# PSUM tiles of one bank for the weighted sums and the final apply, and a re-dealt tail, in a fused attention-convolution and whitening kernel

## The chip, the cores and the metric

The kernel runs on one core of one Trainium2 chip. The core has five engines with a queue of instructions each, which run side by side and wait for each other by semaphores: PE (TensorE, matrix multiplications and transposes), DVE (VectorE), ACT (ScalarE), POOL (GpSimd) and SP (SyncE, used here to issue transfers). PE writes its results to PSUM, which DVE and ACT read; a PSUM bank holds 512 float32 values on each of the 128 partitions. Transfers between the chip's memory (DRAM) and the on-chip SBUF run on 16 DMA engines.

The metric is the time of one execution on the device in microseconds (us). Everything is computed in float32.

## The reference

```python
def _L0_conv_ref(x, w1, b1, w2, b2):          # x: 4 x 256 x 64 x 64
    k = conv(x, w1, padding=6, rhs_dilation=2) + b1      # 7x7 taps, 256 -> 128 channels
    k = conv(k, w2) + b2                                 # 1x1, 128 -> 49
    attn = softmax(k, axis=1)                            # 49 weights for each pixel
    xp = pad(x, 6)
    shifts = stack([xp[:, :, 2*u:2*u+64, 2*v:2*v+64] for u in range(7) for v in range(7)], axis=1)
    return einsum('bkchw,bkhw->bchw', shifts, attn)      # y: 4 x 256 x 64 x 64

def _L1_conv_ref(X, weight, bias):            # 4 groups of 64 channels
    x = X.transpose(1, 0, 2, 3).reshape(4, 64, -1)       # m = 4*64*64 pixels
    xc = x - x.mean(-1, keepdims=True)
    Sigma = 1e-5 * I + einsum('gdm,gem->gde', xc, xc) / m
    rTr = 1.0 / trace(Sigma);  Sigma_N = Sigma * rTr;  P = I
    for _ in range(5):
        P = 1.5 * P - 0.5 * (P @ P @ P) @ Sigma_N
    return (P * sqrt(rTr)) @ xc * weight + bias          # back in NCHW order
```

The first layer computes 49 weights for every pixel and takes the weighted sum of the 49 neighbours. The second needs the mean and covariance of the whole first layer's result before it can write a single output value.

## The kernel before, in words

**Sub-images.** With a dilation of 2, pixels of even and odd rows and columns don't meet. The kernel splits the four images by row parity and column parity into 16 sub-images `n` (0 to 15; `LAST` is 15) of 32 x 32 pixels and 256 channels. The channels are held as two halves `cc` of 128.

**The long first part (to about 310 us and beyond).** The 7x7 convolution is done by a fast transform: DVE forms transformed inputs (`xh`, with the pivot update `ct<-rb`), PE multiplies them (`cv<-xh,wr`, L603, the largest group of the profile; direct rows at L770), DVE and ACT collect (`pv`, `zz`). Softmax follows on ACT and DVE. ACT copies the weights into `zt` (L1126), POOL's queue stores them to DRAM as `sd` (L1145), and SP's queue loads them back as banded matrices `band` and `bandz`, so that a weighted sum becomes a matrix multiplication.

**One sub-image.** `make_blocks` transposes x on PE (L1251) and copies the blocks to SBUF (`xb`, L1282, with edges `xbz`, L1273). `weighted_sum` multiplies blocks by bands into `y` in PSUM (L1320), in two halves of 16 rows, each in five pieces for each `cc`. `store_y` adds a shift and stores y into the place of x (`slot`; ACT at L1342, DVE at L1338). `turn_y` transposes the stored y back (PE, L1399) and copies it to `yt` (ACT, L1409). `moment` multiplies `yt` by itself into the sums `sig` (PE, L1418), from which the covariances come. The methods `first_half` and `second_half` interleave these steps for two neighbouring sub-images, and a plan interleaves them with the convolution of later images.

**The last sub-image** goes in parts, so that channel half 0 is whole early: `store_part` (ACT L1360, DVE L1356), `turn_part` (PE L1368, copies L1377) and `moments_part`. What remains of channel half 1 lies in a list, `units`, of small pieces of PE work.

**Whitening.** `whiten(cc)` is a generator of some eleven steps: trace and mean, then four iterations (the first of the five is in closed form), each of them a multiplication (L1708 through `parts_mm`), a copy `sq` out of PSUM (`evict`), a second multiplication, and DVE's update of `Pm`. The chain for `cc` 0 calls `fill()` between its steps; each call pops a unit onto PE. The chain for `cc` 1 runs later, one step for each tile of the apply loop from tile 4 on (`LEAD`).

**Apply.** 33 output tiles (31 of 512 KB, two half ones at the start): for each, PE multiplies y by the whitening matrix into two PSUM tiles (`parts_mm`, L1708), ACT (L1837) and DVE (L1843) evict one each with scale and shift into `out` (six buffers), and SP issues the transfer (L1849). `bank_pairs` deals the PSUM tiles in turn from three places: pool `ps_y` (one tile of two banks, `apply`), `cv_buf` (two tiles of one bank) and pool `ps_tp` (two of three tiles of one bank).

**Order.** PE's order is the order of the program. On the other engines a scheduler places instructions by priority and by when their inputs come; `high_priority` moves one forward and `issue_after` ties it behind another. Dependences are kept tile by tile. Thus `ps_y`, one buffer of two banks, held both channel halves (or, in `LAST`, both row halves) of y at once.

Of the kernel before, what the change touches and what calls it, by code (L numbers as in the profile page):

```python
# [9 lines left out]
F32 = mybir.dt.float32  # L10
AF = mybir.ActivationFunctionType
# [12 lines left out]
INF = 6  # L24
# [8 lines left out]
def kernel(  # L33
# [71 lines left out]
    ps_tp = ctx.enter_context(tc.tile_pool(name="ps_tp", bufs=3, space=bass.MemoryType.PSUM))  # L105
    ps_y = ctx.enter_context(tc.tile_pool(name="ps_y", bufs=1, space=bass.MemoryType.PSUM))
    ps_sg = ctx.enter_context(tc.tile_pool(name="ps_sg", bufs=1, space=bass.MemoryType.PSUM))
# [702 lines left out]

    acc = ps_y.tile([P, 2, Q8, W], F32, tag="y", name="acc")
    nc.vector.memset(acc, 0.0)
    rows = [(0, br) for br in (1, 2, 3)]
# [40 lines left out]
    def direct0(br, sr):  # L854
        if br in xrs:
            gb = gb5 if br == 5 else gbr
            direct(
                0, br, sr, conv_psum() if br == 5 else acc[:, sr],
                [gb[:, v, :, sr] for v in range(KS)], xrs[br],
            )  # L860
        else:
            u = KS - 1 - 4 * sr - (3 if br == INF else 0)
            w = [tap[:, UPOS[u], v] for v in range(KS)]
            direct(0, br, sr, conv_psum() if br == INF else acc[:, sr], w)

# [96 lines left out]

    direct(1, INF, 0, acc[:, 0], [tap[:, UPOS[3], v] for v in range(KS)])
    prepare(NR0, 1)
# [332 lines left out]
    def weighted_sum(n, half, k, ccs=range(NCC)):  # L1297

        m = PIECES[half][k]
        if n < LAST:  # L1300
            if k == 0:
                y = ps_y.tile([P, NCC, HALF, SW], F32, tag="y", name=f"y_{n}_{half}")
                for cc in ccs:
                    y_ps[n, half, cc] = y[:, cc]
        elif (half, k) == (0, 0):
            y = ps_y.tile([P, 2, HALF, SW], F32, tag="y", name=f"y_{n}_{ccs[0]}")
            for o in range(2):
                y_ps[n, o, ccs[0]] = y[:, o]
        xb = blocks[n, m]
# [34 lines left out]

    y_dve, y_act = {}, {}

    def store_part(half, cc, both=True):

        yt, pc = where(LAST)
        shift = pivots[place(LAST)[1]][:, cc : cc + 1]  # L1350
        ps = y_ps.pop((LAST, half, cc)).rearrange("p r (h c) -> p h r c", h=2)
        for h in range(2):
            o = halves(yt)[:, cc, h, half * HALF : (half + 1) * HALF, bass.ds(pc, TC, 2)]
            with tc.high_priority():
                if h and both:
                    y_dve[LAST, half] = nc.vector.tensor_scalar(  # L1356
                        o, ps[:, h], shift, None, ALU.add
                    )
                else:
                    y_act[0] = nc.scalar.activation(o, ps[:, h], AF.Identity, bias=shift)  # L1360

    def turn_part(half, cc, to=None, on=(nc.scalar.copy, nc.vector.tensor_copy)):

        yt, pc = where(LAST)
        t = tp()
        for k in range(4):
            pe(
                nc.tensor.transpose(  # L1368
                    t[:, k * P : (k + 1) * P],
                    tile_of(yt, cc, 2 * half + k // 2, k % 2, pc),  # L1370
                    turned_by(LAST),
                )
            )
        to = cc if to is None else to
        for k in range(2):
            with tc.high_priority():
                on[k](  # L1377
                    yt_buf[k][:, :, to, :, :GW],
                    t[:, k * C : (k + 1) * C].rearrange("p (h g c) -> p h g c", h=2, c=GW),
                )  # L1380
        turned_part[half, cc] = [yt_buf[k][:, h, to] for k in range(2) for h in range(2)]

    turned_part = {}

    def moments_part(half, cc, pieces=range(4), end=False):

        for k in pieces:
            moment(turned_part[half, cc][k], cc, end and k == 3)

# [270 lines left out]
    sums(0, 0, 3, 4)  # L1660
    store_part(0, 0)
    make_blocks(LAST, 3, y_dve[LAST, 0])
    moments(prev, 1)
    root = work.tile([P, 1], F32, tag="root", name="root")
    with tc.issue_after(y_act[0].ins):
        nc.scalar.activation(root, cmask[:, :1], AF.Sqrt)
    turn_part(0, 0)
    sums(1, 0, 0, 1, 2, 3, 4)
    store_part(1, 0)
    moments_part(0, 0)  # L1670
    turn_part(1, 0)
    sums(0, 1, 0, 1)
# [3 lines left out]
        lambda: sums(0, 1, 2, 3),  # L1676
        lambda: (sums(0, 1, 4), store_part(0, 1, False)),
        lambda: sums(1, 1, 0, 1, 2),
        lambda: sums(1, 1, 3),
        lambda: (sums(1, 1, 4), store_part(1, 1)),  # L1680
        lambda: turn_part(0, 1),
        lambda: turn_part(1, 1, 0, [nc.vector.tensor_copy] * 2),
        lambda: moments_part(0, 1, (0, 1)),
# [29 lines left out]
    def whiten(cc):  # L1713
# [4 lines left out]

        def evict(o, i):
            (nc.vector.tensor_copy if cc else nc.scalar.copy)(o, i)  # L1720

        G = sig[:, cc]
# [10 lines left out]
        nc.vector.tensor_scalar(dg, dg, 1.0 / NPIX, EPS, ALU.mult, ALU.add)  # L1733
        nc.vector.scalar_tensor_tensor(dg, mu, nmu, dg, ALU.mult, ALU.add)
        fill()
# [7 lines left out]
        S = PS[:, 1]  # L1743
        nc.vector.scalar_tensor_tensor(S, G[:, :GW], 1.0 / NPIX, eps, ALU.mult, ALU.add)
        nc.vector.scalar_tensor_tensor(S, t[:, :GW], mu, S, ALU.mult, ALU.add)
# [5 lines left out]
        Pm = PS[:, 0]  # L1751
        nc.vector.scalar_tensor_tensor(Pm, S, -0.5, i15, ALU.mult, ALU.add)
        fill()
        yield

        for it in range(1, T_ITERS):
            t = tp()
            parts_mm(t[:, : 2 * GW], Pm, PS.rearrange("p a c -> p (a c)"))
            sq = rpool.tile([P, 2, GW], F32, tag="sq", name=f"sq{cc}_{it}", bufs=2)
            evict(sq.rearrange("p a c -> p (a c)"), t[:, : 2 * GW])  # L1760
            fill()
            yield
            t = tp()
            parts_mm(t[:, :GW], sq[:, 0], sq[:, 1])
            nc.vector.tensor_scalar(Pm, Pm, 1.5, None, ALU.mult)
            nc.vector.scalar_tensor_tensor(Pm, t[:, :GW], -0.5, Pm, ALU.mult, ALU.add)
            fill()
            yield
# [8 lines left out]
        qi = work.tile([P, 1], F32, tag="qi", name=f"qi{cc}")  # L1777
        nc.vector.reciprocal(qi, q)
        nc.vector.scalar_tensor_tensor(q, qi, rtr, q, ALU.mult, ALU.add)
# [24 lines left out]
    def bank_pairs():  # L1804
        while True:
            t = ps_y.tile([P, 2, NT], F32, tag="y", name="apply")
            yield [t[:, k] for k in range(2)]
            yield cv_buf
            yield [tp(), tp()]
# [3 lines left out]
    for cc in range(NCC):  # L1813
        for b in (3, 2, 1, 0):
# [3 lines left out]
            for k, (r0, nr) in enumerate(rows):  # L1818
# [4 lines left out]
                for pr in range(2):  # L1823
# [5 lines left out]
                        crossed=pr == 1,  # L1829
                    )  # L1830
                if idx > LEAD + 1:
                    next(chains[1], None)
# [51 lines left out]
```

## Time and profile before

| what | value |
|---|---|
| time, median of 3 runs | 682.76 us (682.63, 682.76, 684.98) |
| profiled execution, its own time | 683.23 us |
| its span (first to last instruction) | 681.3 us |
| mean PE clock granted | 0.996 |
| PE busy | 648.7 us, 95% of the span |
| DVE, ACT, POOL busy | 568.4 (83%), 330.4 (48%), 117.2 us (17%) |
| DMA moved | 126.09 MB, mean 185 GB/s |
| output transfers, 512 KB each | 31, 5.0 us from issue to landing in the median |
| first output transfer issued | 635.87 us |

The page's times are microseconds from the start of the span. A line of a timeline reads: start, duration, engine, source line, operation, output<-input, partitions x elements and type, count, and in brackets how long the engine sat idle before it and what ended that. A line of the waits reads: the waiting group <- what it waited for: total, times, longest. The profiled execution is one of its own, and its time lies 0.47 us above the median of the three runs.

### The profile page before, as it was taken

The numbers are of one execution on the slowest core, as the hardware profiler recorded it, in microseconds if no ns is written. First come the engines' busy times: TensorE is split into PE (matmuls) and PEld (weight loads), VectorE is DVE, ScalarE is ACT, GpSimd is POOL, SyncE is SP. The second block draws the span as 40 slices with busy tenths as digits, with TensorE's granted clock in tenths as the row PEclk, the third lists the DMA queues.
The fourth block names the chain that finished last, engine by engine and source line by source line (L and its number), as shares of the span: only waits on it lengthen the run. The fifth ranks groups of instructions, "written<-read, shape, count | busy, mean of one in ns | idle before, by whom it ended". The sixth has DMA issues, their size and how long they took to land.

```text
span 681.3 us, 19062 instructions
## 1 busy us (share of the span) xinstructions
PE 648.7 (95%) x7800; PEld 527.3 (77%) x7800; DVE 568.4 (83%) x1248; ACT 330.4 (48%) x857; POOL 117.2 (17%) x177
## 2 busy tenths in 40 slices
PE   6999999999999999999899999999999999999993
PEld 1439573357899998889899998999899989997421
DVE  2699999899489889999999589989998987634773
ACT  1424340023565565566755555373854656534563
POOL 0000551652213020001022020002220203400000
PEclk9999999999999999999999999999999999999998
DMA  8961999992599979322587484026373325648698
GB/s 318 245 162 67 141 280 349 226 182 33 132 198 222 226 156 361 126 69 74 166 270 250 134 297 166 2 67 190 104 190 109 70 63 138 169 101 362 241 391 357
DMA packets 110607, 126.09 MB, mean 185 GB/s; under 512 B 69255, under 2 KB 91896, under 8 KB 109368
## 3 DMA queue, kind: packets, MB, share of 16 engines
q1 hardware_dynamic: 93528, 69.03, 35.2%
q0 software_dynamic: 10944, 37.57, 21.9%
q10 hardware_dynamic: 6048, 18.27, 8.5%
q8 instruction: 61, 1.00, 0.6%
q14 instruction: 26, 0.21, 0.1%
HBM read 78.78 MB, written 52.36 MB: 192 GB/s over the span
## 4 chain that ended last, share of the span: by engine, by line
PE 66%; DVE 20%; ACT 6%; DMA 4%; issue 2%; POOL 0%; ACTq 0%; SPq 0%; DVEq 0%; POOLq 0%
PE cv L603 22%; PE y L1320 11%; PE cv L770 8%; PE acc L770 8%; PE sig L1418 4%; PE tp L1399 3%; PE tp L1251 3%; DVE pv L352 2%; DVE zz L352 2%; PE cv L251 2%; DVE xh L352 2%; DMA out_dram<-out 2%; DVE ct L352 2%; DVE zz L348 1%; ACT d L1048 1%
## 5 line engine op out<-in xcount | busy, mean ns | idle before, releaser
L603 PE MATMUL cv<-xh,wr 128*49 128x128 f32 x4160 | 232.5, 273 | 0.3 <-ACT pv L614 0.2
L603 PEld LDWEIGHTS cv<-xh,wr 128*49 128x49 f32 x4160 | 226.1, 124 | 3.4 <-issue 1.0
L1145 POOL DMA_DIRECT2D sd<-zt x124 | 65.2, 533 | 334.2 <-ACT zt L1126 268.9
L1320 PE MATMUL y<-band,xb 128*128 128x209 f32 x448 | 94.0, 342 | 5.0 <-ACT xb L1282 2.7
L1320 PEld LDWEIGHTS y<-band,xb 128*128 128x128 f32 x448 | 75.7, 190 | 6.5 <-ACT xb L1282 3.3
L614 ACT COPY pv<-cv 113x486 f32<-113x486 f32 (+2 forms) x60 | 26.0, 433 | 86.4 <-PE cv L603 82.2
L352 DVE SCALAR_TENSOR_TENSOR pv<-pv 113x162 f32<-113x162 f32 x176 | 53.4, 325 | 2.1 <-ACT pv L614 1.3
L1126 ACT COPY zt<-d 32x112 f32<-32x112 f32 (+2 forms) x132 | 38.6, 292 | 15.5 <-DVE d L996 9.9
L1409 ACT COPY yt<-tp 128x512 f32<-128x512 f32 x60 | 35.0, 593 | 19.4 <-PE tp L1399 19.0
L1399 PE MATMUL tp<-ident,slot 128*128 128x128 f32 x240 | 41.5, 296 | 1.2 <-ACT slot L1342 1.2
L1048 ACT ACTIVATE d<-tp,mx 128x49 f32<-128x49 f32 x96 | 27.5, 323 | 28.3 <-DVE mx L1045 28.3
L1251 PE MATMUL tp<-ident,slot 128*128 128x128 f32 x256 | 40.5, 282 | 0.0
L1399 PEld LDWEIGHTS tp<-ident,slot 128*128 128x128 f32 x240 | 34.9, 205 | 6.3 <-issue 3.7
L1418 PE MATMUL sig<-yt 128*64 128x65 f32 x1024 | 38.1, 225 | 1.5 <-ACT yt L1409 1.5
L1251 PEld LDWEIGHTS tp<-ident,slot 128*128 128x128 f32 x256 | 38.2, 204 | 0.2 <-issue 0.2
L1418 PEld LDWEIGHTS sig<-yt 128*64 128x64 f32 x1024 | 33.0, 137 | 6.5 <-ACT yt L1409 2.2
L352 DVE SCALAR_TENSOR_TENSOR xh<-ct 128x512 f32<-128x512 f32 x40 | 26.7, 696 | 10.0 <-PE cv L603 9.8
L1282 ACT COPY xb<-tp 128x512 f32<-128x512 f32 x52 | 30.7, 589 | 8.8 <-PE tp L1251 5.6
L770 PE MATMUL acc<-slot,tap 128*49 128x256 f32 (+7 forms) x224 | 34.7, 468 | 0.0
L770 PEld LDWEIGHTS acc<-slot,tap 128*49 128x49 f32 x224 | 16.1, 123 | 17.9 <-issue 15.5
L147 POOL DMA_DIRECT2D slot<-in_x_dram x12 | 20.4, 1699 | 54.6 <-DVE xh L352 38.2
L348 DVE TENSOR_TENSOR pv<-pv 113x162 f32<-113x162 f32 (+1 forms) x77 | 27.7, 369 | 0.3
(259 smaller groups left out, 1144.4 us busy)
## 6 DMA issues: line engine op xcount, KB each, us to landing
out_dram<-out SPq DMA_DIRECT2D x31, 512.0 KB, 5.0
band<-sd SPq DMA_DIRECT2D x64, 242.0 KB, 3.5
sd<-zt POOLq DMA_DIRECT2D x124, 77.0 KB, 3.1
wr<-gd ACTq DMA_DIRECT2D x14, 588.0 KB, 5.2
wr<-gd ACTq DMA_DIRECT2D x14, 490.0 KB, 4.8
slot<-in_x_dram POOLq DMA_DIRECT2D x12, 512.0 KB, 10.4
ahead<-in_x_dram POOLq DMA_DIRECT2D x12, 512.0 KB, 7.7
spill<-slot POOLq DMA_DIRECT2D x3, 2048.0 KB, 10.7
```

Of the source, the lines that this page charges most:

```text
L348: return in_turn(TT(o, a, b, ALU.subtract))
L352: return in_turn(STT(o, a, f, b, ALU.mult, ALU.add))
L603: nc.tensor.matmul(o, wv[:, sc, sr, cc], xv[bc][:, h * NCC + cc], start=(j == 0), stop=(j == len(terms) - 1), skip_group_check=True,)
L770: nc.tensor.matmul(ps[h * HB : h * HB + KT, :, o0:o1], w[v][:, cc], rhs, start=(j == 0 and k == 0), stop=(j == len(order) - 1), skip_group ...
L1048: nc.scalar.activation(d[:, h, i], t[:, i % NI, h, :KT], AF.Exp, bias=mx[:, i, h : h + 1], accum_out=s[:, h, i : i + 1],)
L1126: ins = nc.scalar.copy(o, i)
L1145: dma = queue.dma_start(bass.AP(tensor=D.tensor, offset=D.offset + h * HS + g * RS, ap=[[LS, TC], [CR * RS, NCH], [1, KS * WS]],), zt[p0 : ...
L1251: nc.tensor.transpose(t[:, h * C + cc * P : h * C + (cc + 1) * P], tile_of(xt, cc, t8, h, pc), turned_by(n),)
L1320: nc.tensor.matmul(y_ps[n, half, cc][:, q0 : q0 + nq, c0:c1], xb[:, cc * P : (cc + 1) * P], rhs, start=(k == 0), stop=(k == len(PIECES[hal ...
L1399: nc.tensor.transpose(t[:, h * C + cc * P : h * C + (cc + 1) * P], tile_of(yt, cc, t8, h, pc), turned_by(n),)
L1409: return nc.scalar.copy(yb.rearrange("p h a g c -> p (h a g) c")[:, :, :GW], t[:, : 2 * C].rearrange("p (e c) -> p e c", c=GW),)
L1418: nc.tensor.matmul(sig[g * GW : (g + 1) * GW, cc], yb[:, g, :GW], yb[:, g], start=(count[0] == 0), stop=end, skip_group_check=True,)
```

## The change

It does five things.

1. `ps_y` has two buffers of one bank instead of one of two. Each y (row half, channel half) and each apply tile of that pool is a tile of its own; so are the two accumulators `acc` of the direct rows.
2. In the last sub-image each bank's y is stored by one engine in one instruction: ACT, and DVE for (1,1). Before, ACT took one half of the columns and DVE the other.
3. A turned block is two transposes in a tile of its own with one copy, not four transposes and two copies by two engines. Each `turn_part` has two parts k; the second is copied by DVE in channel half 0, and all four of channel half 1 by ACT.
4. `units` therefore has 13 entries instead of 11. The chain of `cc` 0 pops the first eleven; the last two, the moments of (1,1), are popped behind the apply tiles 1 and 2.
5. In the whitening chains three small DVE instructions are tied to an order (`traced`, `first`), and the `sq` copies of `cc` 1 go from DVE to ACT.

```diff
-    ps_y = ctx.enter_context(tc.tile_pool(name="ps_y", bufs=1, space=bass.MemoryType.PSUM))
+    ps_y = ctx.enter_context(tc.tile_pool(name="ps_y", bufs=2, space=bass.MemoryType.PSUM))
...
-    acc = ps_y.tile([P, 2, Q8, W], F32, tag="y", name="acc")
-    nc.vector.memset(acc, 0.0)
+    acc = [ps_y.tile([P, Q8, W], F32, tag="y", name=f"acc{sr}") for sr in range(2)]
+    for a in acc:
+        nc.vector.memset(a, 0.0)
...
     def weighted_sum(n, half, k, ccs=range(NCC)):
-        if n < LAST:
-            if k == 0:
-                y = ps_y.tile([P, NCC, HALF, SW], F32, tag="y", name=f"y_{n}_{half}")
-                for cc in ccs:
-                    y_ps[n, half, cc] = y[:, cc]
-        elif (half, k) == (0, 0):
-            y = ps_y.tile([P, 2, HALF, SW], F32, tag="y", name=f"y_{n}_{ccs[0]}")
-            for o in range(2):
-                y_ps[n, o, ccs[0]] = y[:, o]
+        for cc in ccs if k == 0 else ():
+            y_ps[n, half, cc] = ps_y.tile(
+                [P, HALF, SW], F32, tag="y", name=f"y_{n}_{half}_{cc}"
+            )
...
-    def store_part(half, cc, both=True):
+    def store_part(half, cc, on_dve=False):
...
-        ps = y_ps.pop((LAST, half, cc)).rearrange("p r (h c) -> p h r c", h=2)
-        for h in range(2):
-            o = halves(yt)[:, cc, h, half * HALF : (half + 1) * HALF, bass.ds(pc, TC, 2)]
-            with tc.high_priority():
-                if h and both:
-                    y_dve[LAST, half] = nc.vector.tensor_scalar(
-                        o, ps[:, h], shift, None, ALU.add
-                    )
-                else:
-                    y_act[0] = nc.scalar.activation(o, ps[:, h], AF.Identity, bias=shift)
+        i = y_ps.pop((LAST, half, cc)).rearrange("p r (h c) -> p h r c", h=2)
+        o = halves(yt)[:, cc, :, half * HALF : (half + 1) * HALF, bass.ds(pc, TC, 2)]
+        with tc.high_priority():
+            if on_dve:
+                return nc.vector.tensor_scalar(o, i, shift, None, ALU.add)
+            return nc.scalar.activation(o, i, AF.Identity, bias=shift)
 
-    def turn_part(half, cc, to=None, on=(nc.scalar.copy, nc.vector.tensor_copy)):
+    def turn_part(half, cc, k, to=None, on=nc.scalar.copy):
...
         t = tp()
-        for k in range(4):
+        for h in range(2):
             pe(
                 nc.tensor.transpose(
...
-        for k in range(2):
-            with tc.high_priority():
-                on[k](
-                    yt_buf[k][:, :, to, :, :GW],
-                    t[:, k * C : (k + 1) * C].rearrange("p (h g c) -> p h g c", h=2, c=GW),
-                )
+        yb = yt_buf[k][:, :, cc if to is None else to]
+        with tc.high_priority():
+            on(yb[:, :, :, :GW], t[:, :C].rearrange("p (h g c) -> p h g c", h=2, c=GW))
...
-    store_part(0, 0)
-    make_blocks(LAST, 3, y_dve[LAST, 0])
+    stored = store_part(0, 0)
+    make_blocks(LAST, 3)
...
-    turn_part(0, 0)
+    turn_part(0, 0, 0)
+    turn_part(0, 0, 1, on=nc.vector.tensor_copy)
...
-    turn_part(1, 0)
+    turn_part(1, 0, 0)
+    turn_part(1, 0, 1, on=nc.vector.tensor_copy)
...
     units = [
         lambda: sums(0, 1, 2, 3),
-        lambda: (sums(0, 1, 4), store_part(0, 1, False)),
+        lambda: (sums(0, 1, 4), store_part(0, 1)),
         lambda: sums(1, 1, 0, 1, 2),
         lambda: sums(1, 1, 3),
-        lambda: (sums(1, 1, 4), store_part(1, 1)),
-        lambda: turn_part(0, 1),
-        lambda: turn_part(1, 1, 0, [nc.vector.tensor_copy] * 2),
+        lambda: (sums(1, 1, 4), store_part(1, 1, True)),
+        lambda: turn_part(0, 1, 0),
+        lambda: turn_part(0, 1, 1),
+        lambda: turn_part(1, 1, 0, 0),
+        lambda: turn_part(1, 1, 1, 0),
         lambda: moments_part(0, 1, (0, 1)),
         lambda: moments_part(0, 1, (2, 3)),
         lambda: moments_part(1, 1, (0, 1)),
...
-        def evict(o, i):
-            (nc.vector.tensor_copy if cc else nc.scalar.copy)(o, i)
...
-        nc.vector.scalar_tensor_tensor(dg, mu, nmu, dg, ALU.mult, ALU.add)
+        traced = nc.vector.scalar_tensor_tensor(dg, mu, nmu, dg, ALU.mult, ALU.add)
...
-        nc.vector.scalar_tensor_tensor(S, G[:, :GW], 1.0 / NPIX, eps, ALU.mult, ALU.add)
+        with tc.issue_after(traced.ins):
+            nc.vector.scalar_tensor_tensor(S, G[:, :GW], 1.0 / NPIX, eps, ALU.mult, ALU.add)
...
-        nc.vector.scalar_tensor_tensor(Pm, S, -0.5, i15, ALU.mult, ALU.add)
+        first = nc.vector.scalar_tensor_tensor(Pm, S, -0.5, i15, ALU.mult, ALU.add)
...
-            evict(sq.rearrange("p a c -> p (a c)"), t[:, : 2 * GW])
+            nc.scalar.copy(sq.rearrange("p a c -> p (a c)"), t[:, : 2 * GW])
...
-        nc.vector.reciprocal(qi, q)
+        with tc.issue_after(first.ins):
+            nc.vector.reciprocal(qi, q)
...
     def bank_pairs():
         while True:
-            t = ps_y.tile([P, 2, NT], F32, tag="y", name="apply")
-            yield [t[:, k] for k in range(2)]
+            yield [ps_y.tile([P, NT], F32, tag="y", name="apply") for _ in range(2)]
...
+                if idx in (1, 2):
+                    units.pop(0)()
                 if idx > LEAD + 1:
                     next(chains[1], None)
```

## The prediction

> **What bounds the kernel now.** I read the page's totals and slices first, then its chain that ended last, then the waits of PE and the timeline over the last 65 us, where the change does its work, and the windows by stage.
>
> ```profile
> span 681.3 us, 19062 instructions
> ...
> PE   6999999999999999999899999999999999999993
> ...
> DMA  8961999992599979322587484026373325648698
> ...
> PE 66%; DVE 20%; ACT 6%; DMA 4%; issue 2%; POOL 0%; ACTq 0%; SPq 0%; DVEq 0%; POOLq 0%
> ...
> PE y L1320 <- ACT slot L1360: 0.7, 1, 0.7
> ```
>
> PE is at 9 tenths nearly everywhere and its waits are small (the one shown is 0.7 of 681). Only the last slices change the limit: PE falls to 3 and DMA rises to 8. Around 625 to 650 two limits must be kept apart, PE's and the queues'.
>
> ```profile
> 625.88 0.46 PE L1320 MATMUL y<-bandz,xbz 128*128 128x96 f32 x2 [0.67 <-ACT slot L1360]
> ...
> 627.01 0.44 PE L1708 MATMUL tp<-PS 64*64 64x128 f32 x4
> ...
> 628.74 0.44 PE L1708 MATMUL tp<-PS 64*64 64x128 f32 x4
> ...
> 630.72 0.43 PE L1708 MATMUL tp<-PS 64*64 64x128 f32 x4
> ...
> 632.24 0.44 PE L1708 MATMUL tp<-PS 64*64 64x128 f32 x4
> ...
> 633.89 0.41 PE L1708 MATMUL apply<-slot,PS 64*64 64x256 f32 x2
> ...
> 634.70 0.56 ACT L1837 ACTIVATE out<-apply,ab 128x256 f32<-128x256 f32 x1 [0.73 <-PE apply L1708]
> ...
> 635.30 0.54 DVE L1843 TENSOR_SCALAR out<-apply,ab 128x256 f32<-128x256 f32 x1 [0.81 <-ACT out L1837]
> ...
> 635.87 39.74 SPq L1849 DMA_DIRECT2D out_dram<-out  x33
> ```
>
> The last sums on PE, the four whitening iterations of the first channel half (starts 627.01, 628.74, 630.72, 632.24), the first apply tile at 633.89, its two evictions one after the other, and the first output transfer at 635.87. From there:
>
> ```profile
> 630.00:634.70 4.70, 4.62 (x75) 3.54 (x75) 2.63 (x11) 1.04 (x4) 0.00 (x0) 1.00 0.02 3
> ...
> 637.00:639.00 2.00, 1.97 (x20) 0.51 (x16) 1.64 (x3) 1.09 (x2) 0.00 (x0) 1.00 1.04 400
> ...
> 641.00:643.00 2.00, 1.05 (x13) 0.20 (x11) 1.93 (x7) 1.09 (x2) 0.00 (x0) 1.00 1.02 408
> 643.00:645.00 2.00, 2.00 (x24) 0.67 (x20) 1.54 (x5) 1.22 (x3) 0.00 (x0) 1.00 0.95 369
> ...
> 647.00:649.00 2.00, 1.77 (x20) 0.41 (x13) 1.98 (x6) 1.45 (x2) 0.00 (x0) 1.00 0.78 307
> ```
>
> (Columns: stretch, length, busy PE, PEld, DVE, ACT, POOL, then PE clock, DMA share, GB/s.) The output is 16.78 MB; at 408 GB/s a 512 KB tile takes 1.28 us. The queues are idle until 635.87 and then full to the end except where share is under 1: about 0.4 us in 647–649 and about 0.9 in the rest of 637–649, 1.3 in all. So the end is set by the first transfer's start, plus 41 us of data, plus 1.3 us of hunger. A later eviction that is only faster brings nothing.
>
> **The change part by part.** The profiled execution took 683.23 us, span 681.3 and 1.9 around it, 0.47 above the median of 682.76. I subtract gains from 683.23 and move the result by 0.47.
>
> *One tile per bank.* In this trace two accesses to one tile wait for each other even in different banks: sums of (half 1, channels 1) write bank 1 and wait 0.67 for ACT's reading of bank 0; DVE's apply eviction at 635.30 starts when ACT's ends, while a later pair in two separate tiles starts at 635.85 and 636.22. The Trainium skill, "PSUM — Partial Sum Buffer", section "PSUM bank collisions raise a hardware error", keeps two engines apart by bank and 32-partition quadrant, not by tile. By it the order kept between banks is needless; the order within a bank stays, and there two halves on ACT and DVE never overlapped:
>
> ```profile
> 620.42 0.49 ACT L1360 ACTIVATE slot<-y,pivot_x 128x256 f32<-128x256 f32 x1 [1.22 <-PE y L1320]
> ...
> 620.95 0.48 DVE L1356 TENSOR_SCALAR slot<-y,pivot_x 128x256 f32<-128x256 f32 x1 [1.21 <-ACT slot L1360]
> ```
>
> 1. Stores of sub-images up to 12 can begin after channels 0's last matmul, 0.29 to 0.35 earlier, but the ACT store pair ends with the later matmul. PE waits for them at L1399 1.2 in all: I give 0.16 (579.4) and 0.15 (598.8), and at 611.2, where DVE's store stood behind ACT's 0.73, 0.20. Beyond that it is covered by PE's own sums.
> 2. Half 1's store of channels 0 becomes one ACT operation, 0.73 as the 128x512 row at 610.46, in place of 0.49 + 0.04 + 0.48: transposes behind it begin 0.2 earlier (the 0.2 of step 1 moves ahead of it: PE then is 0.4 earlier at its turned block).
> 3. The 0.67 wait goes. With steps 1 and 2 the first iteration starts at 625.86 for 627.01: 1.15 gained.
> 4. The turned blocks become four units of two transposes (0.37 of PE each, half of the 0.74 blocks). The two 0.74 fills stood in iteration 2, which took 1.98; with 0.37 it becomes as long as iterations 3 and 4 (1.52), say 1.48, bound by matmul, ACT copy, matmul, DVE. Iteration 1 stays at 1.73, on PE. Another 0.5; the first apply at about 632.15 (1.7 earlier). Four turned copies on ACT (128x256, 0.375 each at L1377) lie beside: ACT is busy 1.04 of 4.70. If one lands ahead of an iteration's copy, it costs up to 0.37.
> 5. First tile's evictions side by side: 0.55 to 0.6. The first transfer at about 633.6: 2.25 earlier in all.
> 6. Moments of (1,1), eight matmuls of 0.36 to 0.45 in two units, now stand behind apply tiles 1 and 2 on PE; waiting behind them are tile 2's and 3's matmuls, so evictions and transfer 2 come 0.36 later. I estimate 0.6 of hunger after tile 1, where before had 0.5 at 639. On the other hand pairs evict side by side, and whitening 1's four copies (0.28) leave DVE, busy 1.98 of 2.00 in 647–649, for ACT, 1.45. Price from −1.0 (nearly all hunger gone) to +1.0 (a new hole, and sq copies that queue behind ACT's output that waits for an out buffer). My count gives −0.45; as the trace doesn't show these orders, I take 0.
> 7. The traced, `qi` and S orders are of DVE operations of about 0.1 beside PE work, in whitening 0 covered by sums on PE: 0; without cover 0.1 to 0.2.
>
> *Side effects in the body*, from the order of both built programs. Earlier stores let the scheduler move neighbours. ACT: two zt copies (L1126, 0.31 each) now go ahead of the two yt copies (L1409) in half 1 of sub-images 1 and 9. PE waits there already:
>
> ```profile
> 247.31 1.17 PE L1418 MATMUL sig<-yt 128*64 128x65 f32 x32 [0.43 <-ACT yt L1409]
> ...
> 332.66 0.98 PE L1320 MATMUL y<-band,xb 128*128 128x209 f32 x4 [1.39 <-DMA band<-sd]
> ```
>
> Stores begin 0.35 earlier and two copies cost 0.62, so 0.28 more at 247 and as much at 388. DVE: near 310 one pivot update (1.14) goes behind the softmax scaling, so that terms, their POOL stores and SP's band loads leave 0.62 earlier; PE waits for those at 329.83 (0.93) and 332.66 (1.39), so 0.62 is gained. SP: one weight load goes behind two stores near 240, 1.6 later with 12 of slack: 0. POOL's queue is unchanged. Sum with step 1's 0.31: 0.37 gained, between −0.6 and +0.9.
>
> Sum: 2.25 + 0 + 0.37 = 2.6. Profiled 680.6, median **680.2**.
>
> *A rule that speaks against it.* The PE clock is 1.00 in every stretch above, also where PE was busy 1.05 of 2.00. The skill's "TensorE: Matmul & The Clock Gate", section "A second HAM failure mode: psum-queue depth-cycling", describes a kernel that cycled through banks and whose small idles between groups of matmuls made the clock fall to half and back. More one-bank tiles are more such cycling. By the rule nine chain matmul groups of 0.37 to 0.44 could double, 0.4 × 9 = 3.6, and the sum would be 1.0 slower. By the row it is 0. I take the row.
>
> **The rivals.** *A: the sum above*, 680.2.
>
> *B: hunger ends too.* Of 1.3, some 1.0 goes, and the body's 0.56 at 247 and 388 is hidden by slack elsewhere: 682.76 − 2.25 − 1.0 − 0.9 = 678.6. For it: 647–649 is DVE's stretch (1.98 of 2.00), and DVE is relieved. Against it: 643–645 is PE's (2.00), which the change adds to.
>
> *C: gain swallowed.* A transfer earlier at 633.6 meets tile 2 late, the hunger grows by 1, and the reorderings cost 0.6 while the band gain isn't met: 682.76 − 2.25 + 1.0 + 0.2 = 681.7. For it: the transfers then drain sooner than six out buffers fill. Against: in row 637–639 the queues are full even with serial evictions.
>
> *D: slower, whitening 1 sets the pace.* Its steps stand one per tile behind apply matmuls from tile 6 to 16, in order on PE. Its copies now share ACT with output evictions (L1837, 0.78 a tile) that wait for out buffers, so PE stops at the next step, and with it the apply tiles that free them. A step up to 1.28 us is hidden; at 2.1 us eight steps lose 8 × 0.82 = 6.6, less the 2.6: 686.8. Slower than before begins at 1.6 us, by more than noise at 2.03. Against it: ACT is under 1.5 of 2.0 there, and buffers come free only as fast as DMA, which then is the bound anyway.
>
> *E: nothing*, were the order by tile not what held: no; the pairs in separate tiles run side by side. It goes with C.
>
> **How the numbers follow.** A measurement of this kernel can tell about 0.5%, 3.41 us, from no change: faster is below 679.35, slower above 686.17. A 0.53, B 0.26, C with E 0.17, D 0.04. A and C are inside 0.5%, so faster **0.26**, same **0.70**, slower **0.04**. The range runs from **678.4** (B with 0.2 more) to **682.4** (C with 0.7 more of the chain's unknown copies in step 4); it leaves out D, C's worst and B's best.
>
> **What would show it.** Right: first output transfer at about 633.6; PE's wait for ACT's store at the last sums gone; iterations at 1.7, 1.5, 1.5, 1.5; no DVE eviction that waits for ACT's at the same tile; the wait at 332 down by 0.6, those at 247 and 388 up by 0.3. Right for B or C: GB/s in the five stretches from 2 us after the first transfer at 400 throughout, or one of them under 300. Wrong: if the first transfer moved 2.3 but the end did not, hunger took it (C or D: PE's steps at L1708 spaced over 1.6); if it moved by less than 1.5, steps 3 or 4 failed, by an ACT copy in front of an iteration's; if the start of the last 60 us moved by over 0.6, the body was mis-sized.

## The result and the profile after

The changed kernel took 680.79 us in the median of six runs (680.58 to 681.91) beside 683.23 us for the kernel before (six runs). The gain is 2.4 us, or 0.36% of the medians; the ratio on record is 0.9952, with a 95% interval of 0.9933 to 0.9972. So the gain is clear of the scatter, and inside the 0.5% that the prediction calls no change. A second series of runs gave 680.96 (22 runs) beside 683.38 (67 runs), with a ratio of 0.9966 (0.9952 to 0.9980). In four of the traces PE's clock falls to half near 331 us (last section) and its mean is 0.993 or less; runs with such a mean are 1.4 to 2.3 us longer than the others of the same kernel, so the table of the experiments also gives the median of the others.

Predicted were 680.2 and a gain of 2.6. The profiled execution has a span of 678.7, the one that the working gave (683.23 − 2.6 − 1.9). But that the sum is met so closely is luck: two errors cancel. The transfers begin 0.7 us earlier than worked out, and after that 0.7 us is lost that the working put at zero.

The page's totals and slices, then what PE waited for:

```profile
span 678.7 us, 19071 instructions
...
PE   6999999999999999999899999999999999999993
...
DMA  8961899993599979313587485027374325649698
...
PE 67%; DVE 19%; ACT 6%; DMA 4%; issue 2%; POOL 0%; ACTq 0%; DVEq 0%; SPq 0%; POOLq 0%
...
PE sig L1407 <- ACT yt L1398: 2.3, 4, 0.8
...
PE y L1316 <- DMA band<-sd: 1.9, 2, 1.3
```

PE's 0.7 for ACT's store at the last sums is gone from the list. Two that stood there before have changed: the wait of the moments (`sig`) for the turned copies on ACT was 1.5 in four and is 2.3, and the one for the band loads was 2.3 and is 1.9.

The timeline of the changed kernel, PE's first iteration to the first output transfer:

```profile
624.60 0.44 PE L1701 MATMUL tp<-PS 64*64 64x128 f32 x4
...
626.33 0.44 PE L1701 MATMUL tp<-PS 64*64 64x128 f32 x4
...
627.88 0.43 PE L1701 MATMUL tp<-PS 64*64 64x128 f32 x4
...
629.48 0.43 PE L1701 MATMUL tp<-PS 64*64 64x128 f32 x4
...
631.12 0.41 PE L1701 MATMUL apply<-slot,PS 64*64 64x256 f32 x2
...
631.82 0.56 ACT L1830 ACTIVATE out<-apply,ab 128x256 f32<-128x256 f32 x1 [0.61 <-PE apply L1701]
...
631.93 0.54 DVE L1836 TENSOR_SCALAR out<-apply,ab 128x256 f32<-128x256 f32 x1 [0.21 <-PE apply L1701]
...
632.54 19.97 SPq L1842 DMA_DIRECT2D out_dram<-out  x17
```

The iterations start 1.73, 1.55 and 1.60 apart (before 1.73, 1.98, 1.52). DVE's first eviction starts 0.11 behind ACT's instead of 0.60, and waits for PE, no longer for ACT. The first transfer leaves 3.33 us earlier (635.87 before). By stretches, in the columns of the prediction:

```profile
632.40:634.70 2.30, 2.30 (x32) 1.05 (x34) 1.34 (x3) 1.31 (x2) 0.00 (x0) 1.00 0.58 218
634.70:637.00 2.30, 2.30 (x25) 0.77 (x20) 1.65 (x3) 1.72 (x4) 0.00 (x0) 1.00 0.66 261
637.00:639.00 2.00, 2.00 (x20) 0.74 (x12) 1.93 (x8) 1.58 (x3) 0.00 (x0) 1.00 1.01 408
...
641.00:643.00 2.00, 1.80 (x26) 0.61 (x22) 2.00 (x5) 1.21 (x3) 0.00 (x0) 1.00 0.80 303
643.00:645.00 2.00, 2.00 (x24) 0.62 (x20) 1.41 (x4) 1.37 (x3) 0.00 (x0) 1.00 1.01 397
...
647.00:649.00 2.00, 1.93 (x26) 0.81 (x24) 1.51 (x5) 1.37 (x4) 0.00 (x0) 1.00 1.03 412
```

Hunger means time in which the queues have too little to transfer; a stretch with much of it is called a hole below. The hunger at 647 to 649 is gone (0.78 before), but 634.7 to 637 lacks about 0.8 us of transfers (1 − 0.66/1.02 of 2.3) and 641 to 643 about 0.4. From the first transfer to the end of the span it takes 46.16 us, where before it took 45.43. So 3.33 earlier minus 0.73 longer is the 2.6 of the span.

The largest part of the 3.33 that the prediction did not have lies far from the end, at 109 us. PE's timeline before and after:

```profile
96.99 11.55 PE L770 MATMUL acc<-rb,gbr 128*49 128x512 f32 x56
109.22 11.59 PE L770 MATMUL acc<-rb,gbr 128*49 128x512 f32 x56 [0.68 <-ACT zz L782]
```

```profile
96.94 22.92 PE L770 MATMUL acc<-rb,gbr 128*49 128x512 f32 x112
```

Two groups of direct rows write the two accumulators. Before, they were the two banks of one tile, so the second group had to wait for ACT to read the first one's bank. With two tiles the groups run on as one, and the next group (`cv<-slot,gb`) starts at 119.70 instead of 120.63, 0.93 earlier. Of that, 0.05 was there before the wait (96.94 for 96.99) and 0.68 is the wait; the other 0.2 goes with it, since the two groups with their wait took 23.64 us and the one group takes 22.76. It is the same mechanism that the prediction named for the last sums. All other steps together came out 0.2 below their forecast of 2.6 (3.33 − 0.93 = 2.4).

### The profile page after: what moved, and what is told of

It is laid out like the page before. It is cut to its first block, busy times and chain, and to the rows that moved or that the text cites. A ratio compares the mean times of both kernels' runs of the same rounds, so it can differ in the third digit from the quotient of the medians.

```text
span 678.7 us, 19071 instructions
## 1 busy us (share of the span) xinstructions
PE 648.2 (96%) x7800; PEld 527.6 (78%) x7800; DVE 566.3 (83%) x1240; ACT 332.7 (49%) x862; POOL 117.2 (17%) x177
## 4 chain that ended last, share of the span: by engine, by line
PE 67%; DVE 19%; ACT 6%; DMA 4%; issue 2%; POOL 0%; ACTq 0%; DVEq 0%; SPq 0%; POOLq 0%
PE cv L603 24%; PE y L1316 10%; PE cv L770 8%; PE acc L770 8%; PE sig L1407 4%; PE tp L1388 3%; DMA out_dram<-out 3%; PE tp L1252 2%; DVE pv L352 2%; DVE zz L352 2%; PE cv L251 2%; DVE xh L352 2%; DVE ct L352 2%; DVE zz L348 1%; DVE zz L345 1%
## 5 line engine op out<-in xcount | busy, mean ns | idle before, releaser
L770 PE MATMUL acc<-slot,tap 128*49 128x256 f32 (+7 forms) x224 | 34.7, 468 | 0.0
L770 PEld LDWEIGHTS acc<-slot,tap 128*49 128x49 f32 x224 | 16.0, 123 | 18.0 <-issue 15.5
```

The lines of the kernel that those rows point to most:

```text
L770: nc.tensor.matmul(ps[h * HB : h * HB + KT, :, o0:o1], w[v][:, cc], rhs, start=(j == 0 and k == 0), stop=(j == len(order) - 1), skip_group ...
```

## The experiments

Times in the table are medians. The series tells which kernels ran side by side on one chip; the kernel before took 683.44 in series 1, 684.48 in series 2 and 683.38 in series 3, so times of series 2 must not be set against those of the others. Tiles of the apply loop are counted from 0. The last column but one is when DVE has evicted tile 7; the last is what remains from there to the end of the span.

| kernel (series) | median us (runs) | at clock 0.994 and more | first transfer | span | tile 7 evicted | rest |
|---|---|---|---|---|---|---|
| before (1) | 683.44 (23) | 683.38 | | | | |
| before (2) | 684.48 (44) | 683.61 | | | | |
| before (3) | 683.38 (67) | 683.24 | 635.87 | 681.3 | 643.42 | 37.9 |
| changed (3, after_again) | 680.96 (22) | 680.81 | 632.25 | 678.6 | 641.53 | 37.1 |
| acc_joined (1) | 681.69 (14) | 681.55 | 633.70 | 679.6 | 642.61 | 37.0 |
| moments_ahead (1) | 680.55 (5) | 680.48 | 633.17 | 678.5 | 641.27 | 37.2 |
| moments_tile3 (1) | 680.63 (5) | 680.63 | 632.68 | 678.7 | 641.66 | 37.0 |
| pm_first (1) * | 680.96 (10) | 680.66 | 635.12 | 680.9 | 643.83 | 37.1 |
| apply_joined (2) | 681.51 (8) | 681.32 | 633.24 | 679.6 | 641.75 | 37.9 |
| split_only (2) | 680.98 (13) | 680.23 | 633.23 | 678.1 | 640.92 | 37.2 |
| split_again (3) | 680.46 (22) | 680.32 | 633.39 | 678.4 | 641.08 | 37.3 |
| zt_behind (2) * | 684.72 (14) | 683.58 (3 runs) | 636.07 | 682.7 | 645.34 | 37.4 |
| best_ahead (2) * | 683.82 (22) | none | 637.81 | 682.7 | 645.35 | 37.3 |
| zt_sub5 (3) | 680.65 (14) | 680.65 | 631.98 | 678.3 | 641.27 | 37.0 |
| best2 (3) * | 680.33 (22) | 679.97 | 634.81 | 679.7 | 642.36 | 37.3 |

The trace of the kernel before is the one shown ahead of the prediction. An asterisk marks a trace in which PE's clock falls near 331 us; all its times behind that are late, and only differences within it are used.

**Accumulators joined again.**

```diff
-    acc = [ps_y.tile([P, Q8, W], F32, tag="y", name=f"acc{sr}") for sr in range(2)]
+    acc2 = ps_a.tile([P, 2, Q8, W], F32, tag="y", name="acc")    # pool of its own, released later
+    acc = [acc2[:, sr] for sr in range(2)]
```

Expected: 

> The changed kernel with one part undone: the two accumulators of the direct rows are again one PSUM tile of two banks (in a pool of its own, given up before the y tiles are made). Theory (order by tile): PE waits again about 0.7 us for ACT's copy out of bank 0 before it may go on in bank 1 near 109 us, and all behind it is 0.9 later: first output transfer at 633.4 for 632.5, time 681.7 against 680.8 of the changed kernel. Rival (the 0.9 earlier at 120 us came from the memset cut in two, from the loads at the start or from chance): no such wait, 680.8 within 0.3.

Measured: 681.69, which is 1.75 under the kernel before of its series, where the changed kernel has 2.4. The wait is back at its place:

```profile
97.15 11.55 PE L770 MATMUL acc<-rb,gbr 128*49 128x512 f32 x56
109.39 11.59 PE L770 MATMUL acc<-rb,gbr 128*49 128x512 f32 x56 [0.68 <-ACT zz L782]
```

The direct rows of `cv` start at 120.80, 1.10 later than in the changed kernel, and stay 1.1 later to 325 us; the first transfer leaves at 633.70, 1.16 later. Of the 1.10, 0.21 is there at 97 us already, ahead of the wait. PE's, ACT's and SP's orders are the same in both kernels. So 0.7 to 0.9 us of the whole gain is this one wait, and the theory holds.

**The last moments ahead of the apply loop, and behind tile 3.**

```diff
     while 0 not in beta:
         next(chains[0])
+    while units:
+        units.pop(0)()
...
-                if idx in (1, 2):
-                    units.pop(0)()
```

Expected: 

> The changed kernel with the last two units of moments put on PE ahead of apply tile 0 instead of behind tiles 1 and 2. Theory (behind tiles 1 and 2 they hide the start but open a hole in the transfers): first transfer 0.75 later (633.3), the hole before tile 2's transfer shrinks by 0.4, time 681.1 to 681.2, 0.35 over the changed kernel. Rival 1 (the moments cost nothing behind the tiles): 0.75 later, 681.5. Rival 2 (the end is set by supply of whitening 1 further on): 680.8.

```diff
-                if idx in (1, 2):
+                if idx == 3:
+                    units.pop(0)()
                     units.pop(0)()
```

Expected: 

> The changed kernel with both units of moments behind apply tile 3 instead of behind tiles 1 and 2. Theory (the hole of about 0.8 at 635 is half the moments' and half a full tile behind two half tiles): first transfer as before at 632.5, tile 2 and 3 earlier by 0.37 and 0.74, hole down to 0.4, time 680.4. Rival (the hole is due to something else, or opens again at tile 4): 680.8.

Measured: 680.55 and 680.63, both no slower than the changed kernel (five runs each, from another series, in which the kernel before took the same within 0.2). With the moments ahead the first transfer is 0.63 later and the end 0.2 earlier: the hole is worth at least as much as the start. My theory for it had the wrong sign, and rival 2 was nearest. PE's timelines show why. The changed kernel, then the one with the moments ahead, from the first apply matmul to whitening 1's first matmul:

```profile
631.12 0.41 PE L1701 MATMUL apply<-slot,PS 64*64 64x256 f32 x2
...
637.64 0.43 PE L1729 MATMUL tp<-D,blk 128*128 128x64 f32 x2
```

```profile
631.16 0.69 PE L1407 MATMUL sig<-yt 128*64 128x65 f32 x16
631.78 0.43 PE L1701 MATMUL apply<-slot,PS 64*64 64x256 f32 x2
...
637.10 0.43 PE L1729 MATMUL tp<-D,blk 128*128 128x64 f32 x2
```

It is the same set of matmuls. Ahead, the moments cost 0.66 and the seven tiles take 5.32. Between the tiles the whole takes 6.52, which is 0.54 more. With the moments behind tile 3 the hole at 635 is closed (381 GB/s from 635 to 636) and another opens at 638 (258 GB/s), which its rival had as a possibility.

In the changed kernel tile 7 is the last one that the queues wait for: they move 205 GB/s from 642 to 643 and about 400 from then on. For every kernel with split apply tiles the rest column is 36.9 to 37.4 us, whatever happened ahead of tile 7, while the time from the first transfer to the end varies from 44.9 to 46.6. (For the profile of the changed kernel shown above: 641.81 and 36.9.)

That is the main finding on the tail: an earlier first transfer does not by itself bring an earlier end. That the end is set by the last tile that the queues had to wait for fits all these traces, but it is argued from them and not shown alone: a tile nearer to the end must tell the end better, and in split_again and moments_ahead the queues move over 350 GB/s from 640 to 643, so there tile 7 is hardly waited for.

**Whitening 1's first Pm ahead of tile 6's eviction on DVE.**

```diff
                         behind = evicted.get(idx - 1) if idx <= LEAD else None
+                        if idx == LEAD + 2:
+                            behind = firsts[1]        # whitening 1's first Pm
```

Expected: 

> The changed kernel with one order added on DVE: the output eviction of apply tile 6 goes behind whitening 1's first Pm. Theory (the hole at 641 to 643, 0.44 us, is PE's 1.08 wait for Pm, which stands on DVE behind two output evictions of 0.8): the wait falls to 0.3 or less, tile 7's transfer leaves 0.7 earlier, the hole closes, time 680.35. Rival (buffers or queues set the pace there, and the hole only moves to tile 6): 680.8.

Measured: 680.96 over ten runs, as for the changed kernel, and 680.66 for 680.81 in the runs at clock 0.994 and more: 0 to 0.15 us, inside the scatter. The traces of PE of the changed kernel and of this one:

```profile
640.35 0.33 PE L1701 MATMUL tp<-PS 64*64 64x128 f32 x2 [1.08 <-DVE qi L1770]
...
642.82 0.33 PE L1701 MATMUL tp<-PS 64*64 64x128 f32 x2 [0.20 <-DVE PS L1757]
```

```profile
642.21 0.33 PE L1702 MATMUL tp<-PS 64*64 64x128 f32 x2 [0.36 <-DVE PS L1744]
...
644.91 0.33 PE L1702 MATMUL tp<-PS 64*64 64x128 f32 x2 [0.43 <-DVE PS L1759]
```

The wait of 1.08 falls to 0.36, but the next one rises from 0.20 to 0.43, since the eviction that was pushed back now stands before the next update. The time from the first transfer to the end is 45.78 for 46.16. The hole shrinks and moves rather than closes: in half-microsecond stretches the changed kernel lacks about 0.5 us of transfers from 642 to 643.5, and pm_first about 0.35 from 642 to 644.5, which begins with the tile whose eviction was pushed back. So the wait for `Pm` is shown to be a part of the hole at 641, and most of the gain is lost again, as the rival had it. The first line also shows a trap: the releaser is given as `qi`, but `Pm` ended at 640.21 and PE started 0.14 later, the same 0.14 as in the other kernel, where `Pm` is named. `qi` only came last on DVE.

**Apply tiles joined again.**

```diff
-            yield [ps_y.tile([P, NT], F32, tag="y", name="apply") for _ in range(2)]
+            t = ps_ap.tile([P, 2, NT], F32, tag="y", name="apply")   # ps_y released before
+            yield [t[:, k] for k in range(2)]
```

Expected: 

> The changed kernel with one part undone: the apply tiles of the y pool are again one tile of two banks, all else as changed. Theory 1 (the start of the transfers sets the end): the first tile's evictions go one after the other, first transfer 0.5 later (633.1), time 681.3. Theory 2 (the end is set by the tile behind the last hole, tile 7 at 641.8, which PE's wait for Pm sets and not the evictions): first transfer later by 0.5 as well, but time 680.8 to 681.0, unless serial evictions of tile 9 open a later hole as in the kernel before (213 GB/s at 647), then 681.5.

Measured: 681.51, first transfer at 633.24. In the trace the hole at 641 is smaller (332 GB/s from 641 to 642), one of 90 GB/s stands from 637 to 638, and a later one opens at 645 (320 GB/s in that microsecond), which was the condition named for theory 2; the rest behind tile 7 is 37.9, as in the kernel before. The span is 0.9 longer than the changed kernel's, 0.25 of which is there before ACT's first eviction (632.07 for 631.82). What serial evictions cost in time is not shown: the changed kernel did not run in this series, and beside the kernel before of its own series this kernel gains 2.97 (2.29 at clock 0.994 and more), the changed one 2.42 (2.43).

**The split alone.** The kernel before with only the tiles split (the first three hunks of the diff shown, and `bank_pairs`).

Expected: 

> The kernel before with only the tiles split by bank (accumulators, y and apply); the stores, turned blocks, units, the order of the small DVE instructions and the sq copies as before. Theory: the waits for a tile's other bank go (0.9 at 109, 0.7 at the last sums, 0.6 at the first evictions), the ACT reorderings come with it, iteration 2 stays at 1.98 and the last moments ahead of tile 0: first transfer at 633.8, time 681.2, so some 2 of the 2.6 us are the split's alone. Rival (engines by bank and the new units matter as much): 682.0.

Expected of the second run, beside the changed kernel: 

> The kernel before with only the tiles split by bank, once more, beside the changed kernel. Theory 2 (what counts is when tile 7 can leave; first transfer 0.7 later but no hole): equal to the changed kernel or up to 0.5 faster. Theory 1 (first transfer sets the end): 0.7 slower than the changed kernel.

Measured: 680.98 (split_only, beside 684.48 of the kernel before) and 680.46 (split_again, beside 680.96 of the changed kernel and 683.38 of the one before). So it is no slower than the changed kernel; the 0.5 by which it is faster lies inside the intervals (ratios to the kernel before 0.9957, 0.9944 to 0.9970, and 0.9966, 0.9952 to 0.9980). Its first transfer leaves 1.1 later than that kernel's, and from there the queues are fuller, here in split_only:

```profile
634.00:635.00 1.00, 1.00 (x16) 0.72 (x12) 1.00 (x2) 0.78 (x2) 0.00 (x0) 1.00 0.94 350
635.00:637.00 2.00, 2.00 (x23) 1.00 (x14) 1.71 (x7) 1.97 (x5) 0.00 (x0) 1.00 0.95 372
637.00:639.00 2.00, 1.86 (x16) 0.73 (x12) 1.97 (x6) 1.12 (x2) 0.00 (x0) 1.00 1.01 399
641.00:643.00 2.00, 1.93 (x26) 0.73 (x24) 1.61 (x5) 1.37 (x2) 0.00 (x0) 1.00 1.03 403
```

So the split alone brings the whole measured gain; the other parts together (engines by bank, shorter fills, moved moments, `sq` copies on ACT) bring the start forward by some 0.7 to 1.1 us, which the holes take back. In split_only and in moments_ahead PE starts tile 8 at the same time, 639.84, but tile 7 leaves 0.35 earlier in split_only. DVE's evictions of tile 7, first in split_only, then in moments_ahead, show where:

```profile
640.11 0.81 DVE L1838 TENSOR_SCALAR out<-cv,ab 128x512 f32<-128x512 f32 x1
```

```profile
640.46 0.81 DVE L1836 TENSOR_SCALAR out<-cv,ab 128x512 f32<-128x512 f32 x1 [0.28 <-PE tp L1701]
```

In split_only, where the `sq` copies are still DVE's, the eviction follows at once on the small operations of whitening 1; in moments_ahead DVE stands for 0.28 first. That the moved `sq` copies cause this wait is not shown.

**The copies of the terms behind the turned copies.**

```diff
     def finish():
...
         for t8 in (2, 3):
-            turn_y(n, t8)
+            turned = turn_y(n, t8)
+        if n in HELD:                     # (1, 5); in zt_sub5 and best2 (5,)
+            bands(n + 1, turned)
         moments(n, 1)
...
-        bands(n + 1, last)                # end of second_half
+        if n not in HELD:
+            bands(n + 1, last)
```

Expected at both places: 

> The changed kernel with the copies of the terms (zt) of sub-images 2 and 6 emitted behind the turned copies of sub-images 1 and 5, so that on ACT none of them stands in front of those. Theory: PE's two waits at the moments (0.82 at 246.8 and 0.79 at 387.6) fall to about 0.1, everything behind is 1.2 to 1.4 earlier unless the band loads behind the later zt copies take it back; time 679.6. Rival (the gain ends at the next wait for band loads, at 330, so that only the second counts): 680.1. Rival (both are swallowed): 680.8.

Measured: 684.72 beside 684.48 of the kernel before: the whole gain of the change is lost (1.0003, 0.9990 to 1.0015). The waits did fall (0.82 to 0.25 at 246, and 0.79 to 0.25 at the second place), but DVE and ACT then took another order at 305 to 318: two pivot updates went ahead of the softmax scaling, the last `zt` copy ended at 321.5 instead of 320.5, band loads left at 326.8 instead of 325.5, and PE waited 3.70 in one piece instead of 0.65 and 1.30. From the transposes at 327 to the moments behind these sums PE takes 12.8 us instead of 8.3; 1.75 of the 4.5 lost is waiting, and the rest is PE's clock, which is at half there (last section). The edit was not local, so this run says nothing on the wait alone.

Expected at sub-image 5 alone: 

> The changed kernel with the zt copies emitted behind the turned copies at sub-image 5 alone (the wait of 0.79 at 387.6), so that nothing ahead of the band loads at 331 is touched. Theory (a wait behind the last band wait counts in full, one ahead of it is taken by that wait): PE's wait falls to 0.25, all behind it 0.5 earlier, 0.5 under the changed kernel. Rival (the order at 388 is made up elsewhere): no difference.

Measured: the wait at 387 is 0.25 for 0.79; the time is 680.65, 0.3 under the changed kernel where 0.5 was expected. The direction fits, but 0.3 is within the scatter, so a gain in time is not shown.

**Together.** First with the edit at both places:

Expected: 

> Three edits together on the changed kernel: the last moments ahead of apply tile 0, the zt copies behind the turned copies, and tile 6's DVE eviction behind whitening 1's first Pm. Theory 2 (the last hole's end sets the end, and PE's work up to there is the same wherever the moments stand): 680.55 of the moments' move alone, less 0.3 for the hole at tile 7, less 1.2 for the two waits in the body: 679.0. Rival (the body's gain is lost at the band loads): 680.0.

Measured: 683.82 (22 runs) beside 684.48 of the kernel before. As in zt_behind, PE waits long for the bands, here 6.46 in one piece up to 334, and its clock falls to half. Then with sub-image 5 alone:

Expected: 

> The changed kernel with three edits: the last moments ahead of apply tile 0, tile 6's DVE eviction behind whitening 1's first Pm, and the zt copies behind the turned copies at sub-image 5 alone. Theory 2: 0.25 for the first, 0.3 for the second, 0.5 for the third: 1.0 under the changed kernel. Rival (the hole moves on to the next tile and eats the second): 0.7 under it.

Measured: 680.33 beside 680.96 of the changed kernel and 683.38 of the one before (0.9951, 0.9937 to 0.9965), 0.8 under the changed kernel in the runs at clock 0.994 and more. It has the lowest median of its series, by about what the rival gave, though its interval overlaps that of the changed kernel. The split alone, with a far smaller edit, is 0.1 to 0.35 behind it, which is inside the scatter.

## Why the prediction was right, step by step

- *What bounds it*: right in kind (the queues at the end), wrong in the rule. "The end is set by the first transfer's start, plus 41 us of data, plus 1.3 us of hunger" treats hunger as a constant. In the changed kernel the first transfer leaves 3.33 earlier and the end comes 2.6 earlier; the rest was eaten by holes. The 1.3 is also too much by the prediction's own rows: against a full share of 1.02 the stretches at 639 to 641 (0.92 in the trace), 643 to 645 (0.95) and 647 to 649 (0.78) lack 0.8 in all, so rival B had less to win than it was given.
- *One tile per bank*, the reading of the skill's bank rule: right, and split_only shows it alone. The waits between two banks of one tile went at the last sums, at the first evictions and between the two stores. Missed: the accumulators, 0.9 at 109 us, which the diff shows as a split and the list of waits of the kernel before shows as `PE acc L770 <- ACT zz L782: 0.7, 1, 0.7`. I read only the tail for that mechanism. This is the term left out of the sum; acc_joined shows it.
- *Step 1*: 0.16, 0.15 and 0.20 were given, and a little more came. The shift between the two PE timelines grows by 0.21 at 579, by 0.25 at 598 to 600 and by 0.24 at 611 to 614.
- *Steps 2 and 3*: the turned block was to be 0.2 earlier and is 0.18 earlier; the wait of 0.67 was to go, and 0.79 went, of which 0.10 was given back right after. (0.2, 0.2 and 0.67 make 1.07; the prediction wrote 1.15.)
- *Step 4*: 0.5 given, 0.43 measured in iteration 2, and 0.08 lost in iteration 3, where two turned blocks stand now.
- *Step 5*: 0.55 to 0.6 given, 0.56 measured (3.33 at the transfer less 2.77 at the first apply matmul).
- *Step 6*: taken as 0 between −1.0 and +1.0; it was +0.7. The units were sized at their own 0.36 each; between apply tiles the two cost 1.20 together. moments_ahead shows it: there the end comes 45.3 us behind the first transfer, as in the kernel before (45.4). That the sq copies on ACT relieve 647 to 649 is not what the runs show. In split_again, where they are still DVE's, the queues move 401 GB/s in both of these microseconds, and in apply_joined, where they are ACT's, a hole opens at 645. So the split removes that hole.
- *Side effects*: a loss of 0.28 was given for each of the waits at 247 and 388, and 0.39 and 0.40 were measured; a gain of 0.62 was given for the band loads, and 0.37 was measured, with 0.2 or more of scatter from one execution to the next. The sub-image of the second place is 5, not 9 as written.
- *The clock rule*: it was put at 0 for the tail, and the clock there is 1.00 in every stretch in which PE works. The clock does fall in this kernel, at another place and behind longer waits (below).
- *Rivals*: B did not come, since the hunger moved instead of ending; C's mechanism (tile 2 late, hunger up) is what happened, and the unseen 0.9 at 109 us hid it. D did not come: PE's steps are 1.2 us apart at 641 to 648.

## What to carry to other kernels

When tiles are split by bank, search the whole list of waits for pairs on the two halves of one tile, not only the stage that the change is about. In a stage that ends in transfers, look for the last tile that the queues had to wait for and work out when that one leaves; here an earlier first transfer was worth little, because the same engine work still stood before that tile. And try the smallest part of a change alone: here four hunks of it brought all of the gain.

## What the runs showed of the hardware that was not expected

PE's clock halves after waits far shorter than I had thought, and it does so at fixed steps of time. In best2 PE stood idle for 0.96 us before the first band sum at 329.37 and for 1.49 us before the second at 332.30. The windows of that stretch:

```profile
331.00:332.00 1.00, 0.00 (x0) 0.00 (x0) 1.00 (x3) 0.96 (x3) 0.00 (x0) 1.00 1.01 369
332.00:333.00 1.00, 0.70 (x2) 0.69 (x3) 1.00 (x5) 0.20 (x1) 0.00 (x0) 0.51 0.53 112
333.00:334.00 1.00, 1.00 (x5) 0.86 (x4) 1.00 (x4) 0.00 (x0) 0.00 (x0) 0.50 0.88 229
334.00:335.00 1.00, 1.00 (x6) 1.00 (x5) 1.00 (x3) 0.05 (x1) 0.00 (x0) 0.50 0.74 250
335.00:336.00 1.00, 1.00 (x6) 0.97 (x6) 1.00 (x2) 0.96 (x3) 0.00 (x0) 0.79 0.03 12
336.00:337.00 1.00, 1.00 (x9) 1.00 (x8) 1.00 (x4) 0.86 (x2) 0.00 (x0) 1.00 0.00 0
```

The last column but two is the clock: 0.5 from 332.02 to 335.43, in which four sums take 1.76 instead of 0.98 and transposes 1.06 instead of 0.63. That costs some 1.5 us.

The length of the wait does not decide it: in acc_joined a wait of 2.24 at the same place left the clock at 1.00. The traces point to what does. The clock is low for 3.41 us in best2 and pm_first and for 6.83 in zt_behind and best_ahead, and in best2 it falls again at the end of the kernel, at 673.35, 337.92 us after it came back, which is 99 times 3.413. In all fourteen traces the changes of the clock lie whole multiples of 3.413 us apart. So one can lay stretches of this length over each trace and count PE's work in those that end near 331 us:

| trace | stretch | PE busy | clock behind it |
|---|---|---|---|
| zt_behind | 327.14 to 330.56 | 0.70 of 3.41 | 0.50 |
| best_ahead | 326.86 to 330.27 | 0.94 | 0.50 |
| best2 | 328.61 to 332.02 | 1.44 | 0.50 |
| pm_first | 329.09 to 332.50 | 1.45 | 0.50 |
| zt_sub5 | 328.12 to 331.54 | 1.76 | 1.00 |
| changed | 328.70 to 332.11 | 1.81 | 1.00 |
| acc_joined | 328.51 to 331.92 | 2.15 | 1.00 |
| acc_joined | 331.92 to 335.33 | 2.43 | 1.00 |

As far as these traces go, the clock falls behind a stretch in which PE is busy for 1.45 us or less of 3.41 and stays at 1.00 behind one with 1.76 or more. Several short waits in one stretch add up, and a long one that is cut in two by the end of a stretch, as in acc_joined, does no harm. The clock came back behind stretches with 2.85 to 3.41 us of PE's work, and not behind one with 2.43 (zt_behind). The Trainium skill ("TensorE: Matmul & The Clock Gate", Part 1) has a free-running window of about 3.4 us, which agrees; its table lets the clock fall after an idle window, and here one with PE busy for 1.44 us was enough. Since the stretches lie differently in every execution, the same waits can cost 1.5 us in one run and nothing in another. This fits the scatter of the medians above, though for the runs without a trace it is not shown, and it is a reason why a tenth of a microsecond at the band loads can count more than once.
